# Layer 2's mixing with S as the stationary operand, z laid out in zeroed diagonal blocks, and the inverse transform run by channel pairs

## The chip, the cores and the metric

The kernel runs on one core of one Trainium2 chip, in one launch. The metric is device time in microseconds (us); lower is better. The engines are TensorE (PE, with its weight loads listed as PEld), VectorE (DVE), ScalarE (ACT), GpSimd (POOL) and SyncE (SP), which only issues transfers here. A PE matmul takes a stationary operand (`lhsT`, "weights", loaded first) and streams a moving operand (`rhs`) past it; the result lands in PSUM. All matmuls spoken of here are f32, and each f32 matmul appears in the trace as two records, each with its own weight load.

## The reference

The input `x` has shape (16 images b, 16 channels, 256, 256) in f32. Four layers are applied one after the other, each as `x = x + layer(gn(x))`, where `gn` normalises each image over 8 groups of two channels. Layer 0 is a circular 3x3 convolution (written with FFTs), layer 1 a convolution with 5 taps along the diagonal, layer 3 a 3x3 convolution of values quantised to 8 bits with one scale for the whole tensor. The change concerns layer 2, a neural operator in the Laplace domain:

```python
alpha = fft2(x)                                    # b i o x : image, channel, fy, fx
A  = 1 / (omega1[:, None, None, None] - pole1)     # fy  i k p
Bm = 1 / (omega2[:, None, None, None] - pole2)     # fx  i k q
S = einsum('ikpq,oikp,xikq->oxik', residue, A, Bm)
output_residue1 = einsum('biox,oxik->bkox', alpha, S)     # "the mixing"
C = einsum('biox,oikp->bikpx', alpha, A);  D = einsum('bikpx,xikq->bikpq', C, Bm)
output_residue2 = einsum('bikpq,ikpq->bkpq', D, residue)
x1 = ifft2(output_residue1).real                   # "the inverse"
F = einsum('kbpq,bipz->kbiqz', output_residue2, exp(pole1 * ty))
x2 = einsum('kbiqz,biqx->kizx', F, exp(pole2 * tx)).real
out = x1 + x2 / Nx / Ny
```

For each of the 256 x 256 frequencies (fy, fx) the mixing multiplies a complex 16 x 16 matrix S over the channels (i in, k out) with the 16 images' alpha. Because x is real, alpha at (-fy, -fx) is the conjugate of alpha at (fy, fx), so 129 values of fx are enough.

## The kernel before

The program goes through its stages in order: layers 0 and 1 (up to about 1300 us), layer 2's forward transform (1300 to 2245), the mixing (2245 to 3750), the tables of exponentials (3750 to 3836), the inverse (3836 to 4775), layer 3 (4830 to the end). In layer 0 (L410) two tiles `va` and `vb` feed two halves of 64 columns of PE's array; layer 1 is L445.

**Forward transform.** `forth` (L748, L751) transforms along y, `across` (L762 to L778) along x, and `alphad` in DRAM receives the result: per fy, two sign planes h, real and imaginary part r, eight channels i, and then 4 image groups x 129 fx x 4 images in one run. Beside it `sums_over_q` makes `t2`, the sums over the poles q of S: 128 partitions (of input channel, pole and part), and for each half h of the input channels and each output channel k, real and imaginary part for 129 fx, with r outside x.

**Mixing.** `NF` is 64 groups n of four fy. The order of PE, DVE, ACT and POOL in this stage is that of the program text (a hand-written schedule); SP's order is the framework's. `poles(j0)` forms the fractions A for 8 fy on DVE, `masked` spreads them on POOL (L187, tile `l`) into weights, and `system(j0)` forms S for 8 fy: per output channel k and half h one matmul of 128-column weights (8 fy x part x 8 channels) with 258 moving elements of `t2` (L880), after each two k two copies on ACT (L886) into the two tiles `sk`, one per four fy, each copy over 64 partitions with r and x turned round. One step of `system`, that is two matmuls and two copies, is taken after every eight matmuls of the products. `load(n)` brings alpha for four fy as two tiles `zr` (the second with real and imaginary part swapped), by 8 transfers of 258 KB on SP's queue. `spread` turns them into `z` with four masked multiplications per half of fx, shared by DVE and POOL (L911, tables `four`, `four0`): 128 partitions (part, fy, channel), and for each fx four combinations x 16 images. The products (L954) take two neighbouring fx at a time: the weights are `z` of the two (128 columns), the moving operand is `sk` of the two (64 elements), and of the 128 x 64 result only the two diagonal 64 x 32 blocks are used. DVE copies these (L964; L960 for the lone fx = 0) into `ob`, half a tile per group, and `leave` writes 1 MB of `mixd` per group through POOL's queue in one transfer, issued after the next group's first eight products.

**Exponentials.** From 3750 to 3836 us ACT, DVE and POOL make the tables `exps`; PE is nearly idle there.

**Inverse.** The outer loop runs over the 16 images b, the inner over 16 channels k, two at a time. Per pair `ot` comes from `mixd` by four transfers of 128 KB (L1074) and `xt` from `x2d` (L1076), both on SP, and L1078 and L1080 make `fs` for the x2 term. `along_y` is four matmuls of 128-column weights with 128 moving elements (L1033), with a copy to `zt` on ACT (L1036). `along_x` of the channel before follows it on PE: eight matmuls (L1043, L1044), a copy `rq` on ACT (L1046), the sums `w` on POOL and `o` on POOL and DVE (L187), the addition to `xt` with its maximum (L1055) and the statistics (L1058 to L1060) on DVE; after each pair `x3d` is stored through POOL's queue (L1062). Only PE's order is written by hand in this stage.

Of the kernel before, what the change touches and what calls it, by code (L numbers as in the profile page):

```python
# [55 lines left out]
P = 128  # L57
# [13 lines left out]
def constants():  # L71
# [10 lines left out]
    def sin(a, b):  # L82
# [11 lines left out]
    inv = np.stack([np.concatenate([cos(even, m), cos([128], m), sin(even[1:], m)], 0),  # L94
                    np.concatenate([cos(odd, m), sin(odd, m)], 0)], 1)
# [11 lines left out]
    f4, turn_i = p // 8 % 4, np.where(p // 32 % 2 == 0, -1.0, 1.0)  # L107
    four = np.concatenate([1.0 * (f4 == 0) + (f4 == 1), turn_i * ((f4 == 0) * 1.0 - (f4 == 1)),
                           1.0 * (f4 == 2) + (f4 == 3), turn_i * ((f4 == 2) * 1.0 - (f4 == 3))], 1)
    four0 = np.concatenate([1.0 * (f4 == 0), turn_i * (f4 == 1), four[:, 2:]], 1)  # L110
# [5 lines left out]
        "full": full, "inv": inv, "last": last, "four": four, "four0": four0,  # L116
        "not0": 1.0 * (p > 0),
        "strip": strip,
        "chan": p // S == c16,
        "group4": (p % 32 // 4 == q % 32 // 4) / 16.0,  # L120
# [42 lines left out]
def layers(ctx, tc, x, w0, w1, w3, sw, bias, ty, tx, p1a, p1b, p1c, p2a, p2b, p2c, resa, resb,  # L163
# [11 lines left out]
    mixd = dram.tile([N, B, C, N], F32, tag="mixd", name="mixd")  # L175
# [414 lines left out]
    t2 = new(late2, [HC, C, 2, NX], "t2")  # L590
    wy = new(late2, [N], "wy")
    pyr, pyi, py2 = (new(late2, [HC, C], k) for k in ("pyr", "pyi", "py2"))
    mod, four, four0 = table(late2, "mod"), table(late2, "four"), table(late2, "four0")
    blocks = [slice(k * P // 4, (k + 1) * P // 4) for k in range(4)]

    def sums_over_q(pool, psum):
# [30 lines left out]
        for h in range(HC):  # L627
            for k0 in range(0, C, KQ):
# [16 lines left out]
                for k in range(KQ):  # L645
# [4 lines left out]
                    nc.scalar.copy(t2[:, h, k0 + k].rearrange("p r x -> p (r x)"), ps[:, 0 : 2 * NX])  # L650
# [5 lines left out]
        Q.tensor_scalar(t2[:, :, :, 0, 0], t2[:, :, :, 1, 0], -1.0, None, MUL)  # L656
        Q.tensor_copy(t2[:, :, :, 1, 0], a)
# [166 lines left out]
    with ExitStack() as es:  # L824
# [3 lines left out]
        zp = es.enter_context(tc.tile_pool(name="c_z", bufs=2))  # L828
        zr = es.enter_context(tc.tile_pool(name="c_zr", bufs=4))
# [3 lines left out]
        op = es.enter_context(tc.tile_pool(name="c_o", bufs=1))  # L833

        def poles(j0):

            af = new(fp, [HC, 2, C, FC], "af")
            e, g = new(fp, [HC, C, FC], "ae"), new(fp, [HC, C, FC], "ag")
            for h in range(HC):
                tt(V, e[:, h], bc(wy[:, j0 : j0 + FC], 1, C), bc(pyi[:, h], 2, FC), SUB)  # L840
            tt(V, g, e, e, MUL)
            tt(V, g, g, bc(py2, 3, FC), ADD)
            V.reciprocal(g, g)
            for k, at in enumerate(blocks):
                tt(V, af[at, :, 1 - k % 2], e[at], g[at], MUL)
                tt(V, af[at, :, k % 2], g[at], bc(pyr, 3, FC)[at], MUL)
            return af

        KC = 4
        groups = [(j0, k0) for j0 in range(0, N, FC) for k0 in range(0, C, KC)]  # L850
        afs, lss, sks_of = {}, {}, {}

        def masked(g):

            j0, k0 = groups[g]
            ls = []
            for h in range(HC):
                l = new(lp, [2 * KC, 2, 4, 8], f"l{h}")
                for r in range(2):
                    a = afs[j0][:, h, r, k0 : k0 + KC].rearrange("p k (n f) -> p (k n) f", n=2)  # L860
                    tt(Q, l[:, :, r], bc(a, 3, 8), bc(bc(mod, 1, 4), 1, 2 * KC), MUL)
                ls.append(l.rearrange("p (k n) r f i -> p k (n r f i)", k=KC))
            lss[g] = ls

        def system(j0):


            sks = sks_of[j0] = [new(sp, [NX, 2 * C], f"sk{n}") for n in range(2)]
            for k0 in range(0, C, KC):
                g = (j0 // FC) * (C // KC) + k0 // KC  # L870
                if k0 == 2 * KC and j0 + FC < N:
                    afs[j0 + FC] = poles(j0 + FC)
# [61 lines left out]
        for n in range(NF):  # L934
# [34 lines left out]
            if n % 2:  # L969
                for _ in steps:  # L970
                    pass
# [282 lines left out]
```

## Time and profile before

| | us |
|---|---|
| median of three runs (lowest, highest) | 5332.95 (5329.66, 5334.45) |
| the profiled execution: its own time | 5333.26 |
| its span in the trace | 5331.4 |
| busy in the span: PE, PEld, DVE, ACT, POOL | 4863.9, 3862.8, 3589.7, 2994.7, 2865.1 |
| mean granted TensorE clock | 0.959 of full speed |

The span holds all of the execution but 1.9 us. PE is busy for 91% of it, but the stages differ, so the busy time is read stage by stage:

| stage | us | PE | DVE | ACT | POOL |
|---|---|---|---|---|---|
| layers 0, 1 (0 to 1300) | 1300 | 1164 | 857 | 858 | 410 |
| forward (1300 to 2245) | 945 | 873 | 751 | 402 | 496 |
| mixing, its start (2245 to 2289) | 44 | 25 | 28 | 17 | 23 |
| mixing, its loop (2289 to 3749) | 1460 | 1432 | 886 | 1040 | 1119 |
| exponentials (3750 to 3836) | 86 | 2 | 56 | 20 | 16 |
| inverse (3836 to 4775) | 939 | 860 | 677 | 339 | 720 |
| statistics in between (4775 to 4830) | 55 | 14 | 34 | 13 | 26 |
| layer 3 (4830 to 5331) | 501 | 494 | 300 | 305 | 55 |

[...]

### The profile page before, as it was taken

To read this page: it belongs to the slowest core of one execution; us is meant where nothing else is said; L and a number is where in the kernel's file an instruction comes from. 1 tells how busy PE (TensorE), PEld (TensorE's weight loads), DVE (VectorE), ACT (ScalarE), POOL (GpSimd) and SP (SyncE) were. 2 spreads that over 40 slices of the span, in tenths; PEclk is the share of its full clock that TensorE was granted. 3 is DMA by queue.
4 is the path that set the end of the run, shared out by engine and by line. 5 is a ranking of instruction groups with operands and counts; after the bars stand their busy time and mean duration, and the time that the engine had idled before them with its cause. 6 is when DMAs were issued, how large, how long until landed. Compare 5 with 4: busy or idle time off the path is not lost.

```text
span 5331.4 us, 90404 instructions
## 1 busy us (share of the span) xinstructions
PE 4863.9 (91%) x34064; PEld 3862.8 (72%) x34064; DVE 3589.7 (67%) x6683; ACT 2994.7 (56%) x3338; POOL 2865.1 (54%) x3473
## 2 busy tenths in 40 slices
PE   5999999995899899999999999999399999978999
PEld 2555555553899899889999999998388777763444
DVE  4767666766788787766666666664577777776664
ACT  4766776672444344467777777775233333335664
POOL 1332333234455465477777777777277777772110
PEclk9999999997999999999999999998599999999999
DMA  6767776654344444334444444443266666656765
GB/s 143 175 160 169 184 171 159 157 149 118 123 151 152 140 158 156 125 119 141 139 140 139 140 141 141 142 140 125 76 211 214 214 215 216 214 175 266 284 260 201
DMA packets 374627, 885.45 MB, mean 166 GB/s; under 512 B 38320, under 2 KB 238128, under 8 KB 330160
## 3 DMA queue, kind: packets, MB, share of 16 engines
q1 hardware_dynamic: 311728, 577.39, 34.5%
q0 software_dynamic: 62464, 302.29, 19.3%
q8 instruction: 270, 4.42, 0.3%
q14 instruction: 165, 1.35, 0.1%
HBM read 475.84 MB, written 336.07 MB: 152 GB/s over the span
## 4 chain that ended last, share of the span: by engine, by line
PE 57%; DVE 13%; POOL 13%; issue 11%; DMA 4%; SPq 1%; ACT 1%; POOLq 0%; DVEq 0%; ACTq 0%
PE ps_m L954 15%; PE ps L410 12%; PE ps_s L880 8%; PE ps L445 6%; DVE xt L1055 4%; PE ps_a L762 4%; PE ps_y L748 4%; PE ps_y L751 4%; POOL w L187 3%; POOL o L187 2%; PE ps_d L778 2%; POOL x3d L1062 2%; DVE st L1058 2%; DMA zr<-alphad 2%; DVE mn L1060 1%
## 5 line engine op out<-in xcount | busy, mean ns | idle before, releaser
L886 ACT COPY sk<-ps_s 64x516 f32<-64x516 f32 x1008 | 1056.7, 1048 | 400.2 <-PE ps_s L880 390.8
L954 PEld LDWEIGHTS ps_m<-sk,z 128*128 128x128 f32 x8320 | 1036.0, 197 | 84.9 <-DVE ob L964 20.3
L954 PE MATMUL ps_m<-sk,z 128*128 128x64 f32 x8320 | 1023.0, 278 | 32.7 <-POOL z L911 17.0
L911 POOL TENSOR_SCALAR z<-zr,c_four 128x1040 f32<-128x1040 f32 (+1 forms) x256 | 768.2, 3008 | 246.5 <-DMA zr<-alphad 130.1
L964 DVE COPY ob<-ps_m 64x256 f32<-64x256 f32 x1024 | 433.1, 423 | 554.2 <-PE ps_m L954 542.4
L410 PE MATMUL ps<-va,wt 128*64 128x512 f32 (+1 forms) x1632 | 669.3, 571 | 11.4 <-POOL va L382 9.2
L410 PE MATMUL ps<-vb,wt 128*64 128x512 f32 (+1 forms) x1632 | 667.5, 570 | 4.6 <-DMA vb<-va 4.6
L880 PE MATMUL ps_s<-t,l 128*128 128x258 f32 x2048 | 582.9, 408 | 14.8 <-DVE sk L886 12.2
L753 ACT ACTIVATE y<-ps_y,bc 128x384 f32<-128x384 f32 x512 | 297.2, 581 | 422.3 <-PE ps_y L751 422.3
L248 PE MATMUL ps_c<-q,wt 128*128 128x512 bf16 (+1 forms) x2400 | 504.4, 372 | 24.2 <-POOL wt L187 24.2
L431 ACT ACTIVATE v<-xt,nm 32x2048 f32<-32x2048 f32 x248 | 497.2, 2005 | 9.7 <-PE ps L445 3.5
L445 PE MATMUL ps<-v,w1s 128*64 128x259 f32 x4096 | 480.1, 394 | 11.0 <-DVE v L429 6.7
L1043 PE MATMUL ps_o<-c_last,zt 128*128 128x128 f32 x2048 | 420.2, 287 | 75.0 <-ACT zt L1036 75.0
L1046 ACT COPY rq<-ps_o 128x512 f32<-128x512 f32 x256 | 150.1, 586 | 589.5 <-POOL w L187 568.2
L410 PEld LDWEIGHTS ps<-va,wt 128*64 128x64 f32 x1632 | 223.4, 138 | 311.1 <-issue 283.4
L248 PEld LDWEIGHTS <-wt 128*128 128x128 bf16 x2400 | 232.5, 97 | 296.5 <-POOL wt L187 26.9
L445 PEld LDWEIGHTS ps<-v,w1s 128*64 128x64 f32 x4096 | 336.2, 141 | 132.3 <-issue 22.6
L187 POOL TENSOR_TENSOR w<-rq 128x256 f32<-128x256 f32 x512 | 419.0, 842 | 14.3 <-DMA ot<-mixd 10.6
L880 PEld LDWEIGHTS ps_s<-t,l 128*128 128x128 f32 x2048 | 362.8, 197 | 55.0 <-DVE sk L886 12.8
L1044 PE MATMUL ps_o<-exp,fs 128*128 128x128 f32 x2048 | 396.7, 275 | 0.0
L1043 PEld LDWEIGHTS ps_o<-c_last,zt 128*128 128x128 f32 x2048 | 310.3, 191 | 118.7 <-ACT zt L1036 118.6
L187 POOL TENSOR_TENSOR l<-af,c_mod 128x256 f32<-128x256 f32 x512 | 341.1, 690 | 94.7 <-PE ps_s L880 70.7
(205 smaller groups left out, 9216.9 us busy)
## 6 DMA issues: line engine op xcount, KB each, us to landing
zr<-alphad SPq DMA_DIRECT2D x512, 258.0 KB
xt<-x2d SPq DMA_DIRECT2D x256, 512.0 KB
xt<-in_x_dram SPq DMA_DIRECT2D x256, 256.0 KB
x2d<-x2s POOLq DMA_DIRECT2D x256, 256.0 KB, 5.1
mixd<-ob POOLq DMA_DIRECT2D x64, 1024.0 KB, 8.1
ot<-mixd SPq DMA_DIRECT2D x512, 128.0 KB
x3d<-xt POOLq DMA_DIRECT2D x128, 512.0 KB, 5.2
xt<-x3d SPq DMA_DIRECT2D x64, 1024.0 KB
```

Of the source, the lines that this page charges most:

```text
L187: eng.tensor_tensor(o, a, b, op)
L248: nc.tensor.matmul(o, lhsT=w, rhs=src, start=i == 0, stop=i == len(work) - 1)
L410: nc.tensor.matmul(ps[halves[h], lo:hi, :], lhsT=wt0[:, w, :], rhs=v[:, 2 * t + lo : 2 * t + hi, j : j + N], start=j == 0 and k == 0, stop ...
L431: nc.scalar.activation(to, o.xt[c][q_], AF.Identity, bias=o.g.nm[q_, 1:2])
L445: nc.tensor.matmul(ps[halves[h], k, 0:U], lhsT=o.w1[:, w : w + 64], rhs=v1[:, lo : lo + U], start=first_, stop=not first_)
L880: nc.tensor.matmul(ps[:, d, 0 : 2 * NX], lhsT=ls[h][:, k + d - k0, :], rhs=t2[:, h, k + d].rearrange("p r x -> p (r x)"), start=True, stop ...
L886: copy(to.rearrange("p x (k r) -> p k r x", r=2), ps[64 * n : 64 * n + 64, :, 0 : 2 * NX].rearrange("p k (r x) -> p k r x", r=2))
L911: eng.tensor_scalar(z[:, 0 : x1 - x0, f, :].rearrange("p x (q b) -> p q x b", b=BG), zs[f % 2][:, :, x0:x1], (four if n else four0)[:, f : ...
L954: nc.tensor.matmul(ps[0 : 64 * w, d // 2, 0:w, :].rearrange("p x k -> p (x k)"), lhsT=z[:, x0 + d : x0 + d + w].rearrange("p x f b -> p (x ...
L964: V.tensor_copy(ob[rows_, :, h, :, e : e + 2 * PX - w : 2], ps[64 * w : 64 * w + 64, :, w, :].rearrange("p x (k r) -> p k r x", r=2))
L1043: nc.tensor.matmul(ps[:, a, c, :], lhsT=zt[:, a, c, :], rhs=last[:, c, :], start=True, stop=False)
L1044: nc.tensor.matmul(ps[:, a, c, :], lhsT=fs[:, k, a, :], rhs=exps[1][:, k, c, :], start=False, stop=True)
```

## The change

**S stands.** In the products the operands are exchanged: the weights are `sk` of one fx (32 columns: 16 output channels x part), the moving operand is `z` of that fx. `z` holds the four fy in diagonal blocks: the rows of fy f (16 per h: part x 8 channels) hold alpha only in the columns of f and zeros elsewhere, so one matmul gives four fy x 16 images without mixing them. Its 64 moving elements stand in 16 runs of four, 516 elements apart. The four column groups of the array (columns 0, 32, 64, 96) take fx 1 + at, 33 + at, 65 + at, 97 + at, for at = 0 to 31; fx = 0 goes alone. So 4160 products become 8256, one step of S after each second at.

**z.** There are two fixed tiles, zeroed once at the start (one by DVE, one by POOL), then filled by 8 transfers of 129 KB per group on SP, straight from `alphad` into the diagonal blocks; a small memset on DVE of one column of the block stands ahead of each. The `zr` tiles, `spread` and its tables go. For n = 0, whose fy pair differently, blocks are loaded twice and scaled by `alone`.

**S.** `system(n)` makes S of four fy: weights of 64 columns (fy, part, channel), for the two halves h into partitions 0 to 63 and 64 to 127 of one PSUM tile; 1024 matmuls become 2048 and the copies into `sk` span 128 partitions, half as many. `t2` has r inside x, so that the copy reads pairs. `masked` makes 64-column weights for eight k, and `poles` runs in pieces, one after every fourth at.

**U and W.** The two sign planes' products come out as neighbours; ACT copies the second (`other`), and DVE writes sum and difference into `ob`, two instructions per eight at. For fx = 0 a copy on DVE and eight small POOL instructions follow. `leave` writes two halves of 512 KB, on SP's queue, in the next group's at = 2 and 5. `mixd` becomes [128, 4, C, 2, 2, B, 32].

**Inverse.** The outer loop is over the 8 channel pairs, the inner over the images. `ot` holds 8 images (16 transfers of 256 KB, three buffers); `along_y` is 16 matmuls of 32 columns instead of four of 128, with `inv` in two sign versions; both `along_y` of a pair come before both `along_x` of the pair before.

Two smaller edits are left out below: `t2` is written as [HC, C, NX, 2], and the tables `four`, `four0` give way to `alone`, `imag` and `real`.

```diff
@@ the mixing: system, products @@
+                ls = lss.pop((n, k0))
                 for k in range(k0, k0 + KC, 2):
-                    for h in range(HC):
-                        ps = ps_s.tile([P, 2, 512], F32, tag="ps_s", name="ps_s")
-                        for d in range(2):
-                            nc.tensor.matmul(ps[:, d, 0 : 2 * NX], lhsT=ls[h][:, k + d - k0, :],
-                                             rhs=t2[:, h, k + d].rearrange("p r x -> p (r x)"),
-                                             start=True, stop=True)
-                        for n in range(2):
-                            to = sks[n][64 * h : 64 * h + 64, :, 2 * k : 2 * k + 4]
-                            copy = V.tensor_copy if j0 == 0 and n else nc.scalar.copy
-                            copy(to.rearrange("p x (k r) -> p k r x", r=2),
-                                 ps[64 * n : 64 * n + 64, :, 0 : 2 * NX].rearrange("p k (r x) -> p k r x", r=2))
+                    ps = ps_s.tile([P, 2, 512], F32, tag="ps_s", name="ps_s")
+                    for d in range(2):
+                        for h in range(HC):
+                            nc.tensor.matmul(ps[64 * h : 64 * h + 64, d, 0 : 2 * NX], lhsT=ls[h][:, k + d - k0],
+                                             rhs=t2[:, h, k + d].rearrange("p x r -> p (x r)"), start=True, stop=True)
+                        if d:
+                            copy = V.tensor_copy if n == 0 and k % 4 else nc.scalar.copy
+                            copy(sk[:, :, 2 * k : 2 * k + 4].rearrange("p x (k r) -> p x k r", r=2),
+                                 ps[:, :, 0 : 2 * NX].rearrange("p k (x r) -> p x k r", r=2))
                         yield
...
-            x0, x1 = h * (HX + 1), (HX + 1, NX)[h]
-            z = new(zp, [HX + 1, 4, B], "z")
-            for f in range(4):
-                eng = (V, Q)[f % 2]
-                eng.tensor_scalar(z[:, 0 : x1 - x0, f, :].rearrange("p x (q b) -> p q x b", b=BG), zs[f % 2][:, :, x0:x1],
-                                  (four if n else four0)[:, f : f + 1], None, MUL)
-            return z
+        PX = 32
+        GX = 8
+        def load(n, h, f, to):
+            rows_ = slice(64 * h + 16 * f, 64 * h + 16 * f + 16)
+            nc.sync.dma_start(zs[n % 2][rows_, 4 * to : 4 * to + 4].rearrange("p q x b -> p (q x b)"),
+                              alphad[4 * n + f, h].rearrange("r i q x b -> (r i) (q x b)"))
+        def leave(n, p_):
+            nc.sync.dma_start(mixd[2 * n + p_].rearrange("t k r u b g -> (t k r) (u b g)"),
+                              obs[n][:, p_].rearrange("p u b g -> p (u b g)"))
...
+        zs = [new(zp, [FB, NX, BG], f"z{k}") for k in range(2)]
+        V.memset(zs[0], 0.0)
+        Q.memset(zs[1], 0.0)
+        for h in range(HC):
+            for f in range(4):
+                for to in ((0, 1) if f < 2 else (f,)):
+                    load(0, h, f, to)
...
+        def moves(n, at):
+            if n and at in (2, 5):
+                leave(n - 1, at // 3)
+            if n == 1 and at == 0:
+                Q.memset(zs[0][:, 0:8], 0.0)
+            if n + 1 < NF and at % 3 == 1 and at < 24:
+                part = at // 3
+                h, f = part % 2, part // 2
+                V.memset(zs[(n + 1) % 2][64 * h : 64 * h + 64, 4 * f, 0, 0:1], 0.0)
+                load(n + 1, h, f, f)
...
-                        nc.tensor.matmul(ps[0 : 64 * w, d // 2, 0:w, :].rearrange("p x k -> p (x k)"),
-                                         lhsT=z[:, x0 + d : x0 + d + w].rearrange("p x f b -> p (x f b)"),
-                                         rhs=sk[n % 2][:, base + x0 + d : base + x0 + d + w].rearrange("p x k -> p (x k)"),
-                                         start=True, stop=True)
...
-                        for w in range(2):
-                            e = x0 - first + w
-                            V.tensor_copy(ob[rows_, :, h, :, e : e + 2 * PX - w : 2],
-                                          ps[64 * w : 64 * w + 64, :, w, :].rearrange("p x (k r) -> p k r x", r=2))
...
+            z, sk = zs[n % 2], sks.pop(n)
+            steps = system(n + 1) if n + 1 < NF else iter(())
+            ob = obs[n] = new(op, [2, 2, B, PX], "ob")
+            def product(to, x_):
+                nc.tensor.matmul(to, lhsT=sk[:, x_], rhs=z[:, :, x_], start=True, stop=True)
+            for at in range(PX):
+                if at % GX == 0:
+                    ps = ps_m.tile([P, GX, 4 * B], F32, tag="ps_m", name="ps_m")
+                if at == PX // 2 and n % 2 == 0 and n // 2 + 2 < NF // 2:
+                    coming = poles(n // 2 + 2)
+                moves(n, at)
+                for a in range(4):
+                    product(ps[32 * a : 32 * a + 32, at % GX], 1 + PX * a + at)
+                if at % GX == GX - 1:
+                    v = ps.rearrange("p g (n s b) -> p g n s b", n=2, s=2)
+                    other = gp.tile([P, GX, 2, B], F32, tag="other", name="other")
+                    nc.scalar.copy(other, v[:, :, :, 1])
+                    for u, op_ in enumerate((ADD, SUB)):
+                        tt(V, ob[:, :, u, :, at - GX + 1 : at + 1].rearrange("p n b g -> p g n b"), v[:, :, :, 0], other, op_)
+                if at == GX:
+                    first = slice(0, 32)
+                    pe = ps_m.tile([P, GX, 4 * B], F32, tag="ps_m", name="ps_e")
+                    product(pe[first, 0], 0)
+                    alone_ = gp.tile([P, 2, 2, B], F32, tag="alone_", name="alone_")
+                    V.tensor_copy(alone_[first], pe[first, 0].rearrange("p (n s b) -> p n s b", n=2, s=2))
...
+                if at % 2:
                     next(steps, None)
+                if at % 4 == 2:
+                    next(coming, None)
@@ the inverse @@
-        pairs = mixd.rearrange("(a q s) b k x -> a s q b k x", a=2, s=2)
+        BD = 8
         def along_y(b, k, ot):
             ps = ps_z.tile([P, 2, 2, P], F32, tag="ps_z", name="ps_z")
             for a, c in cells:
-                nc.tensor.matmul(ps[:, a, c, :], lhsT=ot[:, a, k % 2, c * P : (c + 1) * P], rhs=inv[:, a, :],
-                                 start=True, stop=True)
-            zt = zp.tile([P, 2, 2, P], F32, tag="zt", name="zt")
+                for t in range(4):
+                    r, half = t // 2, t % 2
+                    nc.tensor.matmul(ps[32 * t : 32 * t + 32, a, c, :], lhsT=ot[:, a, k % 2, 2 * c + half, r, b % BD],
+                                     rhs=inv[:, a, r], start=True, stop=True)
+            zt = tp.tile([P, 2, 2, P], F32, tag="zt", name="zt")
             nc.scalar.copy(zt, ps)
             return zt
...
+            before = []
+            for k, b in [(k, b) for k in range(0, C, 2) for b in range(B)]:
+                if b % BD == 0:
+                    ot = op.tile([P, 2, 2, 4, 2, BD, 32], F32, tag="ot", name="ot")
+                    for a in range(2):
+                        for d in range(2):
+                            for r in range(2):
+                                for u in range(2):
+                                    nc.sync.dma_start(
+                                        ot[64 * u : 64 * u + 64, a, d, :, r].rearrange("p t b g -> p t (b g)"),
+                                        mixd[64 * a : 64 * a + 64, :, k + d, (r + u) % 2, u, b : b + BD]
+                                        .rearrange("q t b g -> q t (b g)"))
...
+                now = [(b, k_, along_y(b, k_, ot), fs, xt) for k_ in (k, k + 1)]
+                for args in before:
+                    along_x(*args)
+                before = now
```

## The prediction

> **What bounds the kernel now.** I read the shares by slice first, then the chain of work that ended last, then busy time by stage, then the timeline inside two stages. Two lines of the page:
>
> ```profile
> PE ps_m L954 15%; PE ps L410 12%; PE ps_s L880 8%; PE ps L445 6%; DVE xt L1055 4%; PE ps_a L762 4%; PE ps_y L748 4%; PE ps_y L751 4%; POOL w L187 3%; POOL o L187 2%; PE ps_d L778 2%; POOL x3d L1062 2%; DVE st L1058 2%; DMA zr<-alphad 2%; DVE mn L1060 1%
> L886 ACT COPY sk<-ps_s 64x516 f32<-64x516 f32 x1008 | 1056.7, 1048 | 400.2 <-PE ps_s L880 390.8
> L911 POOL TENSOR_SCALAR z<-zr,c_four 128x1040 f32<-128x1040 f32 (+1 forms) x256 | 768.2, 3008 | 246.5 <-DMA zr<-alphad 130.1
> ```
>
> The largest shares of the chain are the mixing's two matmuls, L954 and L880. By stage (PE, PEld, DVE, ACT, POOL busy; clock; DMA share):
>
> ```profile
> 2289.00:3749.00 1460.00, 1431.93 (x10303) 1348.31 (x10302) 886.21 (x1730) 1040.21 (x992) 1119.14 (x808) 0.96 0.42 136
> 3750.00:3836.00 86.00, 2.08 (x3) 0.57 (x3) 56.19 (x19) 20.19 (x9) 15.60 (x3) 0.50 0.18 49
> 3836.00:4775.00 939.00, 860.31 (x6398) 755.43 (x6398) 677.17 (x1512) 339.21 (x638) 720.12 (x884) 1.00 0.67 211
> ```
>
> The mixing loop is the first line: 64 groups of four fy in 1460 us, 22.8 each. The inverse is the third. Inside the mixing (start, busy, engine; an f32 matmul is two records, each with a weight load):
>
> ```profile
> 2619.26 0.74 PEld L880 LDWEIGHTS ps_s<-t,l 128*128 128x128 f32 x4
> 2620.34 0.19 PEld L954 LDWEIGHTS ps_m<-sk,z 128*64 128x64 f32 x2 [0.34 <-issue]
> 2620.57 0.73 PEld L880 LDWEIGHTS ps_s<-t,l 128*128 128x128 f32 x4
> ...
> 2623.22 0.74 PEld L880 LDWEIGHTS ps_s<-t,l 128*128 128x128 f32 x4
> 2623.99 1.97 PEld L954 LDWEIGHTS ps_m<-sk,z 128*128 128x128 f32 x16
> 2625.88 0.19 PEld L880 LDWEIGHTS ps_s<-t,l 128*128 128x128 f32 x1
> ```
>
> From 2623.22 to 2625.88 one undisturbed round, 4 records of L880 and 16 of L954, takes 2.66 us. And in layer 0, whose matmuls fill 64 of the 128 columns of the array:
>
> ```profile
> 1019.41 0.59 PE L410 MATMUL ps<-va,wt 128*64 128x512 f32 x1
> 1019.46 0.59 PE L410 MATMUL ps<-vb,wt 128*64 128x512 f32 x1
> 1019.84 0.59 PE L410 MATMUL ps<-va,wt 128*64 128x512 f32 x1
> ```
>
> A `va` record (columns 0 to 63) and a `vb` record (64 to 127) both go through every 0.43 us. L1078, with 512 moving elements on the full array, takes 1.02 for two overlapping records and starts the next at 0.86: 0.43 each. So two column halves run at once at full rate, 0.84 ns per moving element. L880's 258 elements are then 0.217 a record, four are 0.87 of the 2.66, and L954 costs (2.66-0.87)/16 = 0.112. Its 64 elements need only 0.054: its 128-column weight load binds. Two loads of 64 columns stand 0.055 apart (0.19 for two of 0.135), so 32 columns are about 0.03.
>
> PE's own sum per group is 130 x 0.112 + 32 x 0.217 = 21.5 us, 6% under the 22.8: waits for POOL's `z` and for `zr` are the rest. PE bounds the mixing. In the inverse it does not:
>
> ```profile
> 4301.56 1.42 POOL L187 TENSOR_TENSOR w<-rq 128x256 f32<-128x256 f32 x2
> ...
> 4308.92 1.42 POOL L187 TENSOR_TENSOR w<-rq 128x256 f32<-128x256 f32 x2
> ```
>
> Two channels take 7.35 us there, set by POOL's and DVE's alternation, for which ACT's `rq` waits (562.5 us in the waits of this stage); PE needs 0.86 for L1078, 32 x 0.112 along x and 16 x 0.112 along y, 6.2.
>
> **The change, part by part.** *Products.* 4160 matmuls with 128-column weights become 8256 with 32-column weights and 64 moving elements, dealt round-robin over four column groups. One group sees four records between two pieces of S: 4 x 0.054 = 0.22 us if the four run at once, 0.44 if two do, 0.90 if one does. The nearest row is L410, two halves fully at once, each with its own weights; I take 0.22. The moving operand is now runs of four elements; no row shows that, and it costs nothing to twice the streaming (again 0.44).
>
> *S.* 1024 matmuls of 128 columns become 2048 of 64, in pairs on the two halves. Each piece is one pair, two records per half: 0.44, the same work per group (16 x 0.44 = 6.9).
>
> *Switches.* A group now alternates 16 times between 32-column products and 64-column S. The trace has such a switch once per group, at the lone product: L880's four loads reach the next load in 0.77 without a switch (2623.22) and 1.08 with one (2619.26). Of those 0.31, 0.217 is the last record's stream, under which the load would have lain; 0.09 is new, and the 0.055 load is exposed: 0.15. Back again, 0.23 passes where two loads need 0.11: 0.12. I take 0.14 each way, 0.28 a round (between 0.2 and 0.3). [...]
>
> *Round and group.* 0.22+0.44+0.28 = 0.94; 16 are 15.0; the lone product adds 0.11. S of the next group now ends with the group's last round, so PE waits for the last `sk` copy: 0.17 of pipeline tail (a single L880 record shows 0.38 for 0.217 of stream), some 0.1 of handing over (an estimate), and the copy. That one is half as many instructions over 128 partitions. It writes runs of four where it wrote single elements 128 bytes apart: 0.59 (L1036, 512 contiguous) to 1.05 (L886); about 0.7, so 1.0 in all (0.9 to 1.3). Sum 16.15. PE ran 6% over its sum before; I keep that: 17.1. 64 groups are 1094, less 12 for the last, which makes no S: 1082 against 1460, **-378 us**.
>
> *Other engines, per group, all beside PE's 16.* ACT: 8 copies of 0.6 to 1.05 and 4 of 128x256 at 0.37 (L767): 6 to 10. DVE: 8 sums at 0.42 (PSUM source, 256 elements), up to 0.7 as they write single elements apart, poles as before (3.5, now in pieces), small memsets and a copy: 8 to 10. POOL: the `z` spreads (768 us) go; 8 `l` at 0.69 and 8 small ones of 0.25 to 0.36 make 8. If PE fell under 10, ACT or DVE would bind.
>
> *Queues.* `mixd` moves from POOL's queue to SP's, in two halves, issued in the next group's first rounds, where they wait for the last sums; behind them on SP stand that group's remaining `z` loads, late by 1 or 2 us of some 5 to spare. SP issues 10 x 0.61 = 6 us a group. Loads before: 24 of 258 KB in 49.59 us, 2.07 each. Now 8 of 129 KB: 8 us a group if bytes count, 16.5 if the number counts. I take the first: 105 to 141 GB/s against 211 in the inverse says bandwidth is there.
>
> *Start.* Two zeroings of 8256 elements: no row; by L911's 1024 in 1.0 (DVE) and 3.0 (POOL), 8 and 24 us, partly beside the poles (7 us each) and loads of the present 44 us. Taken at 0 (-5 to +20). `t2`'s 32 copies (0.37) may take twice that, on an ACT 43% busy there: 0.
>
> *Inverse.* Along y, 16 records become 64 in four groups: 16 x 0.109 = 1.75 and two switches: PE 6.5 of the 7.35. The cover is 0.85 us; 0, up to +0.95 a pair (+122) if only two groups run at once. `ot` comes in 4 MB bursts for eight pairs, same bytes, three buffers; packets of 1 KB where 2 KB were, and `xt` of 1 KB flows in this stage already: 0.
>
> Sum on the profiled execution, 5333.26 us (span 5331.4; median 5332.95, no different): **4955**.
>
> **Rivals.** *Two groups at once, not four* (or a moving read at half rate). Round 1.16, group 19.7 x 1.06 = 20.8: -138; inverse +122: 5317. For: no row has four. Against: L410's halves don't disturb each other at all.
>
> *Loads bind.* 8 x 2.07 + 2 x 2 = 20.6 a group: 1318, 5190. For: `zr` already ends 130 us of POOL's waits. Against: half the bytes.
>
> *PE cannot be fed: slower.* A round holds 40 weight loads and matmuls where 16 + 4 records held 40 in 2.66 us; now they have 0.94, 24 ns each. The densest long stretch shown is layer 1 (timeline at 607 us), 76 matmuls and 74 loads in 8.5 us, 56 ns each, and it is explained by its streams, so no row shows more. For a short burst, 6 loads and 4 matmuls after a wait:
>
> ```profile
> 1207.08 0.42 PEld L445 LDWEIGHTS ps<-v,w1s 128*64 128x64 f32 x6
> 1207.08 0.66 PE L445 MATMUL ps<-v,w1s 128*64 128x259 f32 x4
> ```
>
> The loads start within 0.28 us: 28 ns an instruction. The break-even is (21.5-1.1)/16/40 = 32 ns. At 38 ns it is 5510; at 54 ns a round is 2.16, a group 35.7 (+820), and an inverse pair's 196 instructions take 10.6 (+416): 6570. [...]
>
> **How the numbers follow.** Forecast case 0.54, with its own range 4880 (no 6%, start -5) to 5060 (copy 1.05, start +20, 0.1 more a round). Two groups 0.12, spread over 5250 to 5350: 0.06 faster, 0.03 same, 0.03 slower. Loads 0.06. Not fed 0.28, of which a third under 5560. The three runs lie within 0.09%; 0.2% is what a measurement can tell. Faster 0.66, same 0.03, slower 0.31. The range 4880 to 5560 leaves out some 0.2, nearly all of it a PE that is not fed.
>
> **What would show it.** L954's successor: four records, one per column group, starting within 0.06 us and again 0.054 later; rounds of 0.94, groups of 16 to 17; one PE wait of 1 us per group on `sk`; ACT, DVE and POOL each under 65% busy in the mixing; the inverse still 7.35 a pair. I am wrong if matmul starts stand evenly 60 ns or more apart (not fed), at 0.11 per group (two at once), if PE waits for DMA `z`, or if the inverse lengthens.

## The result, and the profile after

The changed kernel takes 4877.45 us (median of four runs, 4873.05 to 4879.58) where the kernel before takes 5333.7; the ratio is 0.9141, with a 95% interval of 0.9125 to 0.9157. The forecast was 4955 with a range from 4880 to 5560: the direction and the mechanism came true, the gain was 456 us instead of 378, and the time lies 2.6 us below the range.

By stage (columns: window, its length, then busy time of PE, PEld, DVE, ACT and POOL, granted clock, DMA share, GB/s), the profile after, with the start of the mixing, its loop, the tables and the inverse:

```profile
2245.00:2279.70 34.70, 11.60 (x68) 6.64 (x68) 27.51 (x42) 2.35 (x4) 18.80 (x19) 0.70 0.53 104
2279.70:3296.00 1016.30, 969.25 (x20544) 480.79 (x20544) 560.95 (x1467) 390.75 (x759) 477.95 (x1012) 1.00 0.47 133
3296.00:3382.00 86.00, 9.34 (x133) 5.96 (x133) 56.72 (x20) 22.52 (x14) 15.15 (x2) 0.54 0.70 152
3382.00:4320.00 938.00, 854.63 (x12412) 704.25 (x12412) 679.25 (x1516) 339.10 (x636) 722.53 (x887) 0.99 0.75 207
```

The loop went from 1460 to 1016.3 us (-443.7) and the start from 44 to 34.7 (-9.3). The tables (86) and the inverse (938 against 939) are as they were. The span, 4875.9, is 455.5 shorter; these two stages make 453 of it.

One end of a group in the timeline after (start, busy time, engine, records; a bracket is idle time and what ended it):

```profile
2598.50 0.43 PE L951 MATMUL ps_m<-z,sk 128*32 128x64 f32 x16
2598.86 0.66 PE L887 MATMUL ps_s<-t,l 128*64 128x258 f32 x4
2600.23 0.43 PE L951 MATMUL ps_m<-z,sk 128*32 128x64 f32 x16 [0.71 <-ACT sk L891]
2600.59 0.66 PE L887 MATMUL ps_s<-t,l 128*64 128x258 f32 x4
2601.18 0.43 PE L951 MATMUL ps_m<-z,sk 128*32 128x64 f32 x16
2601.54 0.66 PE L887 MATMUL ps_s<-t,l 128*64 128x258 f32 x4
```

From one block of products to the next are 0.95 us: 0.36 from products to S and 0.59 from S to products. At the group's end (2598.50 to 2600.23) it is 1.73, because PE waits for the last copy into `sk`. From one such wait to the next are 16.02 us. In the single records the four column groups' matmuls start 7 ns after one another, all four within 21 ns, and the next four 0.055 us after them.

The waits of PE in the whole loop after, a complete list (total us, times, longest):

```profile
PE ps_m L951 <- ACT sk L891: 45.0, 63, 0.7
PE ps_m L951 <- issue: 1.9, 1, 1.9
```

PE waits nowhere for `z`, and the granted clock of the loop is 1.00; it was 0.96 before. The groups of the page that answer to those shown before:

```profile
L951 PEld LDWEIGHTS ps_m<-z,sk 128*32 128x32 f32 x16384 | 281.5, 109 | 444.1 <-issue 369.8
L891 ACT COPY sk<-ps_s 128x516 f32<-128x516 f32 x508 | 299.0, 589 | 453.2 <-PE ps_s L887 415.1
L951 PE MATMUL ps_m<-z,sk 128*32 128x64 f32 x16384 | 444.7, 225 | 47.8 <-ACT sk L891 45.0
```

The copies into `sk` take 0.589 us each over 128 partitions, where they took 1.048 over 64.

### The profile page after: what moved, and what is told of

It reads as the page before. It is cut to its first block, busy times and chain, and to the rows that moved or that the text cites. A ratio compares the mean times of both kernels' runs of the same rounds, so it can differ in the third digit from the quotient of the medians.

```text
span 4875.9 us, 122104 instructions
## 1 busy us (share of the span) xinstructions
PE 4391.2 (90%) x50448; PEld 2939.4 (60%) x50448; DVE 3261.1 (67%) x6410; ACT 2332.2 (48%) x3094; POOL 2208.6 (45%) x3667
## 5 line engine op out<-in xcount | busy, mean ns | idle before, releaser
L887 PE MATMUL ps_s<-t,l 128*64 128x258 f32 x4096 | 672.2, 408 | 19.2 <-POOL l L190 16.5
L190 DVE TENSOR_TENSOR ob<-ps_m,other 128x256 f32<-128x256 f32 x512 | 281.3, 644 | 423.8 <-ACT other L964 413.3
L951 PEld LDWEIGHTS ps_m<-z,sk 128*32 128x32 f32 x16384 | 281.5, 109 | 444.1 <-issue 369.8
L891 ACT COPY sk<-ps_s 128x516 f32<-128x516 f32 x508 | 299.0, 589 | 453.2 <-PE ps_s L887 415.1
L951 PE MATMUL ps_m<-z,sk 128*32 128x64 f32 x16384 | 444.7, 225 | 47.8 <-ACT sk L891 45.0
L190 POOL TENSOR_TENSOR l<-af,c_mod 128x256 f32<-128x256 f32 x512 | 320.2, 654 | 320.1 <-PE ps_s L887 312.4
L1062 PE MATMUL ps_o<-c_last,zt 128*128 128x128 f32 x2048 | 410.4, 282 | 2.5 <-ACT zt L1055 2.5
L1052 PE MATMUL ps_z<-c_inv,ot 128*32 128x128 f32 x8192 | 276.7, 277 | 98.6 <-ACT zt L1055 98.6
L1052 PEld LDWEIGHTS ps_z<-c_inv,ot 128*32 128x32 f32 x8192 | 212.1, 110 | 226.4 <-ACT zt L1055 128.3
```

Of the source, the lines that this page charges most:

```text
L190: eng.tensor_tensor(o, a, b, op)
L887: nc.tensor.matmul(ps[64 * h : 64 * h + 64, d, 0 : 2 * NX], lhsT=ls[h][:, k + d - k0], rhs=t2[:, h, k + d].rearrange("p x r -> p (x r)"), ...
L891: copy(sk[:, :, 2 * k : 2 * k + 4].rearrange("p x (k r) -> p x k r", r=2), ps[:, :, 0 : 2 * NX].rearrange("p k (x r) -> p x k r", r=2))
L951: nc.tensor.matmul(to, lhsT=sk[:, x_], rhs=z[:, :, x_], start=True, stop=True)
L1052: nc.tensor.matmul(ps[32 * t : 32 * t + 32, a, c, :], lhsT=ot[:, a, k % 2, 2 * c + half, r, b % BD], rhs=inv[:, a, r], start=True, stop=True)
L1062: nc.tensor.matmul(ps[:, a, c, :], lhsT=zt[:, a, c, :], rhs=last[:, c, :], start=True, stop=False)
```

## The experiments

### Do four column groups run at once?

One variant deals the products out one column group at a time, another two at a time. The instructions are the same. (All variants ran once, except where a lowest and a highest time are given.)

```diff
-                for a in range(4):
-                    product(ps[32 * a : 32 * a + 32, at % GX], 1 + PX * a + at)
+                for j in range(4):              # one column group at a time
+                    a, g = at % GX // 2, at % 2 * 4 + j
+                    product(ps[32 * a : 32 * a + 32, g], 1 + PX * a + at - at % GX + g)
```

```diff
+                for j in range(4):              # two column groups at a time
+                    i = at % GX * 4 + j
+                    a, g = i // 16 * 2 + i % 2, i % 16 // 2
+                    product(ps[32 * a : 32 * a + 32, g], 1 + PX * a + at - at % GX + g)
```

> The changed kernel, but the 32 products of eight at in the order of the column groups: eight in a row go to the same 32 columns before the next group begins, where the changed kernel deals them round. Same instructions. Theory (four groups stream at once, 0.054 each): 16 records in one group take 16 x 0.054 = 0.86 instead of 0.22 between two pieces of S; a round 1.59, a group 10.4 more, the time 4877 + 64 x 10.4 = about 5540. Rival (the order makes no difference, because loads or the issue of instructions set the 0.36 us from product to S): 4877.

> The changed kernel with its products dealt round two column groups at a time (0 and 32 for sixteen products, then 64 and 96). Theory (each group streams at 0.054 a record beside the others): 8 records per group between two pieces of S, 0.44 instead of 0.22, a group 16 x 0.22 = 3.5 more, the time 4877 + 64 x 3.5 = 5100. It lies a third of the way from the changed kernel to the run with one group at a time. Rival (the penalty of one group at a time came from its single PSUM partition range or its one queue of weights, and two remove it): 4877 to 4950.

Measured: 5549.36 and 5092.31 us, against 5540 and 5100 expected. The timeline with one group at a time, and then with two:

```profile
2562.89 1.08 PE L951 MATMUL ps_m<-z,sk 128*32 128x64 f32 x16
2563.90 0.66 PE L887 MATMUL ps_s<-t,l 128*64 128x258 f32 x4
2564.48 0.24 PE L951 MATMUL ps_m<-z,sk 128*32 128x64 f32 x1
```

```profile
2563.15 0.64 PE L951 MATMUL ps_m<-z,sk 128*32 128x64 f32 x16
2563.72 0.66 PE L887 MATMUL ps_s<-t,l 128*64 128x258 f32 x4
2564.30 0.64 PE L951 MATMUL ps_m<-z,sk 128*32 128x64 f32 x16
```

From the start of a block of 16 records to S are 0.36 us on four groups, 0.57 on two and 1.01 on one. That is 4, 8 and 16 records of 0.054 in a row, and 0.14 more each time; S stays at 0.58. The column groups are the cause: dealt round, four stream at once. With one group the single records follow each other at 0.056 us. So 64 moving elements that are read in runs of four, 516 apart, stream at 0.87 ns each, close to the 0.84 of the contiguous reads of layer 0.

### What does the alternation cost?

Two variants take the steps of S less often, two after every fourth at or four after every eighth; the matmuls are the same. A third cuts the weights of S into 32 columns, so that the tile size never changes.

```diff
-                if at % 2:
-                    next(steps, None)
+                if at % 4 == 3:                 # by two; by four: if at % GX == GX - 1, range(4)
+                    for _ in range(2):
+                        next(steps, None)
```

```diff
-                        for h in range(HC):
-                            nc.tensor.matmul(ps[64 * h : 64 * h + 64, d, 0 : 2 * NX], lhsT=ls[h][:, k + d - k0],
+                        for c in range(2 * HC):
+                            h, half = c // 2, slice(c % 2 * 32, c % 2 * 32 + 32)
+                            nc.tensor.matmul(ps[32 * c : 32 * c + 32, d, 0 : 2 * NX], lhsT=ls[h][:, k + d - k0, half],
```

> The changed kernel, but four steps of S after every eighth at instead of one after every second: the same matmuls, a quarter of the alternations between 32-column products and 64-column S. Theory (each alternation there and back costs PE 0.28 us): a group falls from 16.04 by 12 x 0.28 to 12.7 us, the 63 groups with S by 212, to about 4665. Rival (a round of 0.947 is what its loads and streams need, whatever the order): the group stays at 16.0 and the time at 4877. Second rival (ACT or DVE binds when S comes in bursts): a group of 13.5 to 15, with PE waits for the copies of S.

> The changed kernel, but each 64-column weight tile of S cut into two of 32 columns, so that S runs on the same four column groups as the products: twice as many S matmuls, and no change of tile size in the loop. Theory (the 0.28 a round is the price of changing the tile size, and four groups stream S as fast as two do halves): a round is 0.22 + 0.44 = 0.66, a group 16 x 0.66 + 0.10 + 0.79 = 11.5 us, the time 4877 - 63 x 4.55 = 4590. Rival (the 0.28 belongs to going from one matmul to another operand, not to the tile size): round and time stay, 0.947 and 4877. Rival (four groups cannot stream 258 elements each at full rate): S takes 0.87 a step, a round 1.1 or more, the time 5000 or more.

> The changed kernel with two steps of S after every fourth at: half the alternations. Theory (0.286 for each, as the undisturbed stretches of the run with four steps give it): a group of 16.04 - 8 x 0.286 = 13.75, the time 4877 - 63 x 2.29 = 4733. PE's records then follow at 650 in 13.75 us, 256 in 5.4 us, and if the stalls of the run with four steps (256 records apart, with no wait behind them) come from a supply of instructions of one block of 256 in about 5 us, there are none or few here. Rival (the stalls come from the burst itself, through the copies of S or the PSUM tiles): stalls here too, 4750 to 4780.

Measured: 4743.96 by two (4733 expected), 4694.86 by four (4665), and 4787.41 with S on 32 columns (4590). The undisturbed rounds show the price. By four, and then on 32 columns:

```profile
2572.38 1.10 PE L951 MATMUL ps_m<-z,sk 128*32 128x64 f32 x64
2573.41 1.97 PE L887 MATMUL ps_s<-t,l 128*64 128x258 f32 x16
2575.31 1.18 PE L951 MATMUL ps_m<-z,sk 128*32 128x64 f32 x64
```

```profile
2560.06 0.43 PE L952 MATMUL ps_m<-z,sk 128*32 128x64 f32 x16
2560.28 0.65 PE L888 MATMUL ps_s<-t,l 128*32 128x258 f32 x8
2560.72 0.43 PE L952 MATMUL ps_m<-z,sk 128*32 128x64 f32 x16
2560.94 0.65 PE L888 MATMUL ps_s<-t,l 128*32 128x258 f32 x8
```

By four, what were four rounds of 0.947 take 2.93: three alternations fewer save 0.86, 0.286 each. On 32 columns a round is 0.66, the bare 0.22 + 0.44, so the 0.286 is the price of changing the tile size and not of changing the operand. That run lost most of it again, though. PE's waits in its loop (the largest four lines):

```profile
PE ps_m L952 <- issue: 67.8, 67, 3.2
PE ps_s L888 <- issue: 30.2, 30, 2.5
PE ps_m L952 <- DMA z<-alphad: 25.6, 16, 2.4
PE ps_m L952 <- DVE z L941: 21.3, 13, 2.6
```

Two new limits appear that the changed kernel does not meet. One is `z` that comes late now that groups are shorter, 61 us with the lines that are not shown. The other, 98 us, is time in which PE waited for nothing that the profile shows. Such a stall in the timeline:

```profile
2566.35 0.47 PE L952 MATMUL ps_m<-z,sk 128*32 128x64 f32 x13
2567.79 0.25 PE L952 MATMUL ps_m<-z,sk 128*32 128x64 f32 x2 [0.97 <-issue]
2567.80 0.42 PE L888 MATMUL ps_s<-t,l 128*32 128x258 f32 x3
```

I counted all of PE's records in this loop: matmuls, weight loads and six semaphore instructions a group, which is 778 records a group here and 650 in the other variants. The 89 stalls of 0.5 us or more stand 256 records apart, or a multiple of it, to the record. From 2500 to 2700 us of this run the queue that brings instructions moved (packets, MB, share of the 16 DMA engines)

```profile
q8 instruction: 41, 0.67, 1.6%
```

that is 41 packets of 16 KB, while PE ran 10,685 matmuls and loads, 41.7 times 256. In the whole loop there are 192 packets for 193 blocks of 256, and each of the 89 stalls ends 1.2 to 1.9 us after the end of such a packet. An undisturbed group uses 256 records in 3.8 us here (778 in 11.6). By four (650 in 12.6, 256 in 5.0) has 21 such stalls in its loop, by two (650 in 13.7, 256 in 5.4) has two.

### Is it the supply of instructions?

The variant with S on 32 columns, with the loads of `z` left out after the first three groups, so that later fy are not read:

```diff
-                load(n + 1, h, f, f)
+                if n < 2:
+                    load(n + 1, h, f, f)
```

> The run with S on 32 columns, whose z is loaded for the first three groups of four fy only; all later groups work on what then stands in the two z tiles, so that alpha of later fy is left out. The 1 MB of z and its 8 transfers per group go, those of mixd stay. Theory (PE there outruns the transfers that bring its instructions, one block of 256 records in about 4.9 us, and they share the DMA engines with z): the stalls, 1 to 2.5 us after each 256 or 512 records, become shorter or rarer, and the group falls from 14.5 towards its undisturbed 11.5: 4600 to 4700. Rival (the supply is limited by itself, whatever else the DMA engines do): 4787. Rival (the stalls are waits for something else in the loop, such as copies or l): 4787.

Measured: 4631.9 us, in the expected range. The two loops, with all loads and without (columns as above):

```profile
2282.00:3203.00 921.00, 739.39 (x24515) 599.30 (x24510) 600.94 (x1463) 391.22 (x758) 472.42 (x1010) 0.98 0.53 148
```

```profile
2281.00:3049.00 768.00, 704.20 (x24560) 577.12 (x24552) 599.78 (x1465) 390.99 (x759) 476.55 (x1011) 1.00 0.25 93
```

PE's waits in the loop without the loads (the three largest lines; the rest is 3 us):

```profile
PE ps_m L953 <- ACT sk L892: 44.6, 62, 0.8
PE ps_m L953 <- issue: 11.8, 16, 2.6
PE ps_s L888 <- issue: 3.0, 6, 0.7
```

Of 89 stalls of 0.5 us or more 21 are left, with a median of 0.8 us instead of 1.1, at multiples of 256 records still (768 and 2048 among the distances). Groups without one take 11.6 us, where the sum is 11.5. A packet of instructions takes 1.0 us where it took 1.3 (medians). So in these runs PE's instructions come through the DMA engines in packets of 16 KB, one for each 256 of its records (192 packets for 193 blocks), and a packet takes longer at a DMA share of 0.53 than at 0.25; that the traffic delays them rests on this one variant. The pace of one block in 4.9 us that some expectations take for a limit is the mean distance of the packets from 2500 to 2700 us with the waits for `z` in it; without the loads the packets are 3.9 us apart (median). Of the 153 us the waits for nothing shown make 83 (98 to 15), those for late `z`, which this edit takes away too, 59 (61 to 2); the waits for `sk` grow by 25, and the rest is PE's busy time.

### Where was the 6% of the kernel before?

Half of the loads of alpha are left out of the kernel before, so that the tile with real and imaginary part swapped is never brought and the first is used in its place:

```diff
-            zs = [new(zr, [B // BG, NX, BG], "zr") for _ in range(2)]
-            for k, z in enumerate(zs):
+            zs = [new(zr, [B // BG, NX, BG], "zr")] * 2
+            for k, z in enumerate(zs[:1]):
```

> The kernel before, with half of its loads of alpha in the mixing: the tile with real and imaginary part swapped is left out and the first tile is used in its place (the products are made of the wrong numbers, their count and shape are the same). Theory (PE's 6% over its own sum came from z that waited for late loads, and from the half clock that PE was granted after each such wait): waits and slow stretches go together, the granted clock of the mixing loop rises from 0.96 to 1.00, the group falls from 22.8 to 21.5, the loop from 1460 to 62 x 21.5 + 2 x 14.6 = 1362, the time to about 5235. Rival (the waits alone cost, the clock is lowered by something else, such as steady load): -37, about 5295, clock 0.96 or 0.97. Rival (the 6% lies in PE's matmuls): 5333.

Measured: 5252.6 us, where about 5235 was expected; the kernel before took 5328.78 beside it. The loop falls by 83 us, to 1377, at a clock of 1.00:

```profile
2291.00:3668.00 1377.00, 1376.98 (x10301) 1300.70 (x10301) 876.14 (x1730) 1042.41 (x992) 1131.67 (x808) 1.00 0.35 95
```

The kernel before had these waits of PE in its loop, and then, around one of them (1.35 us, ended at 2606.2), these rows by time, in which the granted clock is the third figure from the end:

```profile
PE ps_m L954 <- POOL z L911: 17.0, 12, 8.0
PE ps_m L954 <- DVE ob L964: 10.9, 5, 2.3
```

```profile
2603.00:2606.00 3.00, 1.86 (x17) 1.72 (x16) 1.91 (x5) 0.48 (x1) 3.00 (x2) 1.00 0.25 105
2608.00:2610.00 2.00, 2.00 (x10) 1.75 (x9) 1.07 (x3) 0.29 (x1) 2.00 (x2) 0.63 0.25 103
2610.00:2614.00 4.00, 4.00 (x17) 3.81 (x17) 0.85 (x2) 1.80 (x2) 4.00 (x5) 0.50 0.26 107
2616.00:2620.00 4.00, 4.00 (x31) 3.83 (x31) 1.31 (x4) 3.00 (x3) 1.21 (x2) 1.00 0.94 246
```

The waits themselves are 28 us. The other 55 of the 83 are the fall of PE's own busy time, 1431.93 to 1376.98: matmuls at half clock after the waits, as in these rows, and in the last groups after the longest wait (8.0 us; clock 0.50 from 3729 to 3749). A clock of 0.96 over 1460 us is 58. With loads that come in time both are gone: PE is busy for all but 0.02 us of the loop, at a clock of 1.00. What is left, 1377, is 15 us over the 1362 of the expectation's sum, and that remainder is not explained.

In this loop the length of a wait does not tell whether the clock halves. These two rows of 20 us (length, busy PE, clock, DMA share, GB/s) lack 2.26 and 0.58 us of PE:

```profile
2549.00:2569.00 20.00, 17.74 (x137) 1.00 0.41 133
2689.00:2709.00 20.00, 19.42 (x126) 0.83 0.35 126
```

### Is there a better place for S, and what hides the inverse?

Two variants take four steps of S earlier (after at = 3, 11, 19, 27), the second also issues the loads of `z` sooner; the by-four variant in its first form was then run again.

```diff
+                if at % GX == 3:
+                    for _ in range(4):
+                        next(steps, None)
-            if n + 1 < NF and at % 3 == 1 and at < 24:      # the second only
-                part = at // 3
+            if n + 1 < NF and at % 2 == 1 and at < 16:
+                part = at // 2
```

> The run with four steps of S after every eighth at, but taken after at = 3, 11, 19 and 27 instead of 7, 15, 23 and 31, so that the last copies of S lie beside the products of the last four at (0.45 us) and the wait of 0.79 at the end of the group falls to about 0.35. By the sums alone a group is 16 x (0.22 + 0.44) + 4 x 0.286 + 0.10 + 0.35 = 12.1 us. Theory (instructions in blocks of 256, one in about 4.9 us): 650 records need 12.4 to 12.7 us whatever the order, so the time gains 20 to 45 on the 4695 of the run before: 4650 to 4675. Rival (no such limit, the stalls belong to the order of that run): 4877 - 63 x 3.94 = 4629. Rival (the new place lets PE wait for l or for a PSUM tile): 4695 or more.

> The run before with S after at = 3, 11, 19 and 27, and the eight loads of z issued at every second at from 1 to 15 instead of every third from 1 to 22. Theory (that run lost its gain to the last loads of z, which had 3.4 us from their issue to the group's end and take about 4 to land; PE waited 1.5 to 2.9 us in most groups and then ran on half the clock): no PE wait on z, clock back at 1.00, group 12.1 by the sums or 12.4 to 12.7 by the supply of instructions, the time 4630 to 4675. Rival (bytes or number of the transfers bind at a group of 12.5 us, whenever they are issued): waits on z stay, 4750 or more.

> The run with four steps of S after every eighth at (7, 15, 23, 31), z loaded as in the changed kernel, once more and timed against the kernel before, since neither later place of S beat its single look of 4694.86. Theory (supply of instructions at 650 records a group, and a last z load with 5.6 us before the group ends): 4690 to 4705, ratio 0.878 to 0.882, few waits on z. Rival (its single look was lucky, waits on z come in other executions as in the two runs with S taken earlier): 4715 to 4760.

Measured: 4849.27 (4842.78 to 4850.46; ratio to before 0.9082, 0.9067 to 0.9098), 4721.37 (4713.7 to 4724.09; 0.8847, 0.8816 to 0.8878), and for by four in its first form 4690.28 (4686.36 to 4692.09; 0.8778, 0.8764 to 0.8793). The first of them, in its loop:

```profile
PE ps_m L951 <- DMA z<-alphad: 60.5, 23, 3.0
PE ps_m L951 <- DVE z L940: 40.9, 15, 3.3
PE ps_m L951 <- DVE ag L852: 37.9, 15, 3.0
```

The theory that an earlier S gains 20 to 45 us fell. The earlier S did remove the wait for `sk`, and with it the time in which the last load of `z` landed: PE waits for that instead, up to 3.3 us a time, and the granted clock of the loop falls to 0.94. (Two of the lines name DVE instructions; the waiting matmul waits for several things, and nearly all of these waits end 0.2 to 0.5 us after a load of `z` has landed.) Loads issued sooner take most of the waits away (31.6 us left from 2300 to 3000), but not all: 4630 to 4675 was expected, and their median landing grows from 3.4 to 5.1 us. Why by four with the late S is still 31 us quicker was not settled. It is the quickest version that leaves nothing out, 187 us under the changed kernel.

The last run gives PE more to do in the inverse, with the 16 matmuls along y on two column groups at a time:

```diff
-            for a, c in cells:
-                for t in range(4):
-                    r, half = t // 2, t % 2
+            for r in range(2):
+                for (a, c), half in [(cell, half) for cell in cells for half in range(2)]:
+                    t = 2 * r + half
```

> The changed kernel with the 16 matmuls of 32 columns along y ordered so that two column groups alternate at a time, not four; nothing else. Theory (PE has a cover of 0.85 us of the 7.35 us that POOL and DVE set for a channel pair in the inverse): 16 x 0.109 = 1.75 more for a pair, 0.9 of it beyond the cover, 128 x 0.9 = 115, the time about 4990. Rival (the inverse hangs on POOL and DVE alone and PE's turn can slide): 4877 to 4900.

Measured: 4874.98 us, where 4990 was expected: no difference. The inverse of this run, same window as above, and one pair along y with the row behind it:

```profile
3382.00:4320.00 938.00, 920.88 (x12391) 799.15 (x12389) 681.70 (x1520) 341.88 (x634) 726.01 (x889) 0.99 0.75 206
```

```profile
3702.75 2.80 PE L1052 MATMUL ps_z<-c_inv,ot 128*32 128x128 f32 x64
3705.48 0.49 PE L1062 MATMUL ps_o<-c_last,zt 128*128 128x128 f32 x2
```

Along y takes 2.73 us a pair in its timeline instead of 1.88; 1.75 more was expected and 0.85 came, and why is open. PE is busy for 921 of 938 us, where it was 855, and the stage is not longer. So the cover is real and at least 0.85 us a pair; what lies beyond it was not reached.

## Why the prediction was right or wrong

**Round: right.** 0.947 against 0.94, and each of its three terms was borne out: products 0.22 on four groups (0.87 with one), S 0.44 on two halves or four quarters, and 0.286 for two changes of tile size, where 0.28 was taken from a single switch per group in the trace before. That row was of tiles of 64 and 128 columns; that 32 and 64 cost the same was assumed, and it came true. In the run with S on 32 columns, where the tile size never changes, a round is 0.66 and the 0.28 is gone.

**End of group: right within 0.2.** 0.79 against 1.0; the copy took 0.589 where 0.7 was assumed. Handing over, put at 0.1 without a row, is 0.07 us before the copy and 0.05 behind it in the timeline after. The group by its own sum was 16.15 and is 16.02.

**The 6%: the step that failed.** "PE ran 6% over its sum before; I keep that" put 0.95 us on each group, 60 us on the loop, and the group has none of it. The text itself had named the cause, "waits for POOL's `z` and for `zr`", and the change takes the `z` work off POOL and `zr` out of the kernel. In the kernel before, loads that came in time took 83 us off the loop; in the changed one the only wait of every group is that for `sk`, and the clock is 1.00. An allowance was carried over whose cause was removed in the same edit. Its size had a second part that was not seen: the 28 us of waits had brought about 55 us of half clock after them. Without the 6% the sum for the loop was 1022, and it is 1016. So of the 77 us between forecast and result the 6% makes some 60, the start 9, the loop's own sum 5. The low end of the range had no 6% and a start 5 us shorter, which together make about 4890, and it was put at 4880; the start and the slightly shorter group took the time just past it.

**Start: 0 taken, -9.3 measured.** The two zeroings took 6.9 (DVE) and 7.0 us (POOL), not 8 and 24. What was not counted is that S for four fy is made ahead of the loop where S for eight was: PE's busy time there falls from 25 to 12 us, ACT's from 17 to 2. That this makes the 9 us is argued from these rows and was not tried.

**Other engines, queues, inverse: right.** In the loop DVE is busy for 55%, ACT 38%, POOL 47%; no wait for `z`; the inverse the same to 1 us. (Of the chain's shares the prediction calls L954 and L880 the largest; by the line it shows, L410 of layer 0, 12%, stands between them. Nothing in its sum hangs on this.)

**The rivals.** Two groups at once was forecast at 5317 with the inverse, 5195 for the mixing alone; dealt two at a time the mixing gives 5092. The 6% (1.1 of its 20.8 us a group, some 70 us) is most of that difference too. "Loads bind" does not hold at 16 us a group, where PE waits nowhere for `z`; in shorter groups late loads do show (3.8 us of waits for `z` from 2300 to 3000 at 12.6 us a group by four, 61 in the loop with S on 32 columns). "PE cannot be fed" did not happen, and it was nearer than the result shows: a round holds 40 records in 0.947 us, 24 ns each, and stalls for instructions, two in the loop at 21 ns a record (by two), are 21 at 19 ns (by four) and 89 at 15 (32 columns). The break-even of 32 ns was met with room of a quarter. PE's waits for nothing that the profile shows are 1.9 us in the loop of the changed kernel and 98 with S on 32 columns. The 20 matmul records of a round in 0.947 us are 47 ns each, and four start within 21 ns, where the prediction named even distances of 60 ns or more as the sign of a PE that is not fed.

## What to carry to other kernels

An excess of measured time over an engine's own sum belongs to its causes: name them, and ask of each whether the change keeps it, before the percentage is carried over. A short wait of PE cost more than itself here where the granted clock halved after it (1.35 us, then some 7 at or near 0.50), and its length alone did not tell whether it would (0.83 over 20 us with 0.58 of waiting, 1.00 with 2.26). When PE works on small tiles, count the changes of tile size (0.14 us each here) and the records per microsecond (42 in a round of the changed kernel; at 67, with S on 32 columns, PE stalled 89 times for 0.5 us or more): both cost time here once the columns had been filled.

## What the runs showed of the hardware that was not expected

Four column groups of 32 stream f32 at once, with moving elements in runs of four, each at the rate of one alone (0.055 us for 64 elements, 0.056 with one group at a time), and their matmuls start 7 ns after one another, four within 21 ns. A change between tiles of 32 and 64 columns and back cost 0.286 us. A wait of 1.35 us was followed by some 7 us at or near a clock of 0.50, and 0.58 us of waiting by a clock of 0.83 over 20 us, while 2.26 us within another 20 us, and 0.71 us at the end of every group after, left it at 1.00. PE stalled at exact multiples of 256 of its records: 89 times for 0.5 us or more in a loop whose undisturbed groups use 256 in 3.8 us, beside 148 GB/s of transfers, and 21 times beside 93 GB/s.
